# Two convolution blocks on one core: weight loads on another queue, an earlier comparison and table, one shared PSUM tile, and a half of the output summed by VectorE

## The chip, the cores and the metric

The kernel runs on 1 core of one Trainium2 chip. The core has TensorE (matmuls, results in PSUM), VectorE (DVE), ScalarE (ACT), GpSimd (POOL) and SyncE (SP), each with its own instruction stream that is executed in order, and 16 DMA engines that all of them share. The engines wait for each other by semaphores. The metric is the device time of one execution in microseconds. It is given as the median of 3 runs: 2735.2 us (2733.67 to 2737.22).

## The reference

The input `x` is 4 images of 256 channels of 48 x 48, float32. Two layers are added to it, each on a group-normalised copy (32 groups):

```python
x = x + _L0_conv_ref(_gn(x), ...)   # layer 0
x = x + _L1_conv_ref(_gn(x), ...)   # layer 1
```

Layer 0 is a 3x3 convolution with batch norm (given statistics) and ReLU, then 8-head attention over the 2304 pixels (32 channels a head, softmax over all pixels) and a projection:

```python
x = relu(bn(conv3x3(Vx, conv_w) + conv_b))
qkv = einsum('oc,bchw->bohw', qkv_w, x) + qkv_b
attn = softmax(einsum('bhdn,bhdm->bhnm', q, k) * scale)
out = einsum('oc,bchw->bohw', proj_w, einsum('bhem,bhnm->bhen', v, attn)) + proj_b
```

Layer 1 makes 45 guidance maps by a 3x3 convolution. In groups of nine, after a softmax, they weigh nine shifted copies of the input, at dilations 1, 6, 12, 24 and 36. The input and the five sums are mixed by a 1x1 convolution (256 x 1536), and the result `y` is normalised per channel with the mean and variance over all four images:

```python
for i, d in enumerate((1, 6, 12, 24, 36)):
    w = softmax(guidance[:, 9 * i:9 * (i + 1)], axis=1)
    outs.append(_dyn_branch(x, w, d))
y = conv1x1(concat(outs), W_scale)
return (y - mean) * rsqrt(var + EPS) * gamma + beta
```

So the output is x1 + (y * ysc + ysh), where x1 is the result of layer 0 and `ysc`, `ysh` are per channel and known only when `y` of all images is done.

## The kernel before, in words

A channel tile is `[128, 2, 2304]`: 128 partitions, two halves of 128 channels (`h` or `o`), all pixels of an image. Everything is float32. A pass over an image is cut into six chunks of 384 pixels.

**The first image.** Lines 557 to 560 issue four DMAs on SP's queue that load image 0 into `x_first`, 576 KB each. After some constants and memsets on POOL, line 2170 begins the first pass: seven DMAs on POOL's queue load the weights (`wc`, the convolution's, in two halves; then `wqkv`, `wp`, `vbc`, `wcat`, `wsc`), and twelve more on the same queue write zeros from `e1` to the margins of `w_d` in DRAM (line 2181). VectorE takes the statistics of the image as it lands (line 655), aggregates them (665), makes two sums on the first half of the weights (`weights.pair`, 786 and 787), and then finishes the group norm: `rstd_of` (97 to 99) adds EPS, ScalarE takes the root, VectorE the reciprocal. The image is normalised into `pads[0]`, the transform of the convolution (847 to 852) follows, and TensorE begins the convolution (962).

ScalarE needs a table for a function; another function can need another table. `table(func)` (line 610) runs the function on one column, so that the table is loaded there.

**The passes.** The loop at 2149 goes over b = 0..4. In pass b the layer 1 work of image b-1 (`dynamic_filters`) is interleaved with the convolution and the q, k, v of image b; then the attention of image b follows. In pass 4 no next image is left: `alone` is true, and the layer 1 work of image 3 is interleaved with `late()`, the 1x1 mixing of two chunks (4 and 3) of image 2 that were put off until then.

**The order within a pass is written by a planner**, at build time. Each piece of work is a generator in a list of streams: `loads`, `far`, `near` (the dilation of 1), `filters` (guidance maps and softmax), `mixes` (the 1x1 convolution), and `other`. A generator yields the time at which its next step is due. `drive` (1961) takes the first stream whose step is due by the planner's TensorE time; when none is due it takes a matmul from `other`. `clock(engine, ns, *after)` adds the cost of a step to an engine's planned time, and `slot(tag, bufs)` gives the planned time at which a buffer is free again. `moved` (1495) gives a copy to ScalarE or VectorE, whichever is free sooner by this plan. What the planner decides is fixed before the kernel runs; the engines then wait for each other by semaphores.

**Late chunks.** `late()` (1912) makes a PSUM tile `both` of two banks for each of the two chunks, in a pool with one buffer; each half gets 12 matmuls and is copied by ScalarE to `yl` (1934). The tile of the second chunk stands in the place of the first.

**The flag.** A bound on the attention scores is kept for each image and half; if one is over SAFE, a general version of the kernel runs afterwards. In pass 4 the stream `filters` calls `flag_of` (2077) before the third set of guidance maps: VectorE compares the bounds (`okay`), TensorE sums them into the PSUM tile `misc`, VectorE reduces them and writes `flag`. `misc` has one buffer, which the guidance maps and their transposes use too.

**The end.** `last_loads` (1944) is a stream that, once the last `near` work is issued, calls `table(AF.Sqrt)` and loads four chunks of `y` of image 2. After the last matmuls `finish` (2087) makes `ysc` and `ysh` (`batch_norm_of`, 161) and then the output, image by image: 0, 2, 3, 1. For images 0 and 1, `near_end` (2096) has ScalarE make y * ysc + ysh for the two parts of a half in place, and VectorE add it to x1; `y` lies by chunks of six rows apart (c, j), x1 by rows (j, c), so that each VectorE part reads from all chunks. For images 2 and 3, `far_end` (2116) has ScalarE shift x1, and VectorE add y * ysc in one scalar_tensor_tensor per chunk. SP issues the stores.

## Time and profile before

| What | Value |
|---|---|
| median of 3 runs (lowest, highest) | 2735.2 us (2733.67, 2737.22) |
| the profiled execution's own time | 2732.03 us |
| its span, first to last instruction | 2730.3 us |
| mean granted TensorE clock | 0.987 |
| first convolution matmul | 21.37 us |
| last matmul begins (four of L1897) | 2691.15 us |
| VectorE's last sum ends | 2722.15 us |

The profile is one execution of the program. The page gives the busy time of the engines and its share of the span; queries of the trace give the instructions in order of time (start, busy time, engine, line, operation, tiles and, in square brackets, the idle time of the engine before it and what ended it), and tables of who waited for whom (total time, how often, longest). A wait for several semaphores is put down to the one that came last. Matmuls are pipelined and their ends are modelled. PEld is TensorE's weight load; SPq is SyncE's queue.

### The profile page before, as it was taken

How to read it: one execution, taken by the hardware profiler on the slowest of the kernel's cores; microseconds unless marked ns; L12 is line 12 of the kernel's file. 1: busy time of each engine (PE TensorE's matmuls, PEld its weight loads, DVE VectorE, ACT ScalarE, POOL GpSimd, SP SyncE). 2: the span in 40 equal slices, each digit the busy share in tenths (PEclk: the TensorE clock that was granted, in tenths of full speed). 3: DMA queues.
4: the chain of work that ended last, by engine and by line, in shares of the span. 5: the costliest groups of instructions: out<-in, count | busy, mean ns of one | idle time of the engine just before them, and what ended most of it. 6: DMA issues, size and time to landing. Idle time of an engine off the chain costs nothing. (4 is left out here: it accounts for less than half of the span.)

```text
span 2730.3 us, 42450 instructions
## 1 busy us (share of the span) xinstructions
PE 2593.3 (95%) x16906; PEld 1091.3 (40%) x16906; DVE 2081.7 (76%) x2014; ACT 1806.0 (66%) x2273; POOL 810.3 (30%) x882
## 2 busy tenths in 40 slices
PE   6999999999999999999999999999989999999994
PEld 5632222555562222355554222245555222235452
DVE  7768888757739898857765988885875988885476
ACT  4479888634449888854446888884344988874344
POOL 5201100477520010068650001017764001000462
PEclk9999999999999999999999999999999999999997
DMA  4804445323252445433324344442325344432465
GB/s 171 225 13 105 108 98 108 90 61 107 63 104 59 99 93 110 99 80 86 90 57 84 86 105 100 102 99 74 94 69 136 99 93 96 103 82 75 114 192 182
DMA packets 137790, 273.67 MB, mean 100 GB/s; under 512 B 58104, under 2 KB 99744, under 8 KB 136688
## 3 DMA queue, kind: packets, MB, share of 16 engines
q0 software_dynamic: 25952, 135.74, 21.8%
q1 hardware_dynamic: 111632, 135.14, 18.6%
q8 instruction: 135, 2.21, 0.3%
q14 instruction: 71, 0.58, 0.1%
HBM read 112.12 MB, written 36.04 MB: 54 GB/s over the span
## 5 line engine op out<-in xcount | busy, mean ns | idle before, releaser
L1374 DVE TENSOR_TENSOR acc<-acc,p 128x2048 f32<-128x2048 f32 (+1 forms) x568 | 1052.1, 1852 | 119.8 <-ACT p L1334 70.0
L1334 ACT ACTIVATE p<-se 128x1536 f32<-128x1536 f32 x648 | 938.1, 1448 | 0.0
L1325 PE MATMUL so<-q,k 32*128 32x512 f32 (+1 forms) x1440 | 728.6, 593 | 18.8 <-ACT p L1333 16.3
L1325 PE MATMUL se<-q,k 32*128 32x512 f32 (+1 forms) x4320 | 737.3, 593 | 0.0
L1359 PE MATMUL num<-p,vT 128*32 128x512 f32 (+1 forms) x5760 | 711.3, 561 | 2.2 <-ACT ao L1384 2.2
L1333 ACT ACTIVATE p<-so 128x512 f32<-128x512 f32 x648 | 388.8, 600 | 193.8 <-PE se L1325 89.1
L1802 POOL TENSOR_TENSOR near<-near,prod 128x384 f32<-128x384 f32 x384 | 386.5, 1039 | 290.6 <-DVE prod L1796 281.7
L1325 PEld LDWEIGHTS so<-q,k 32*128 32x128 f32 x1440 | 216.7, 183 | 535.8 <-ACT p L1333 493.0
L1378 POOL DMA_DIRECT2D ring<-p x124 | 105.5, 851 | 775.2 <-ACT p L1334 486.3
L1359 PEld LDWEIGHTS num<-p,vT 128*32 128x32 f32 x5760 | 136.7, 108 | 480.0 <-issue 449.7
L1796 DVE TENSOR_TENSOR prod<-wb,pad 128x768 f32<-128x768 f32 x192 | 181.8, 954 | 92.3 <-ACT wb L1783 56.0
L1897 PE MATMUL py<-far,wsc 128*128 128x384 f32 x704 | 234.6, 487 | 0.0
L1783 ACT COPY wb<-ws 128x384 f32<-128x384 f32 x216 | 108.5, 506 | 183.1 <-DVE prod L1796 123.7
L1325 PEld LDWEIGHTS se<-q,k 32*128 32x128 f32 x4320 | 227.3, 183 | 4.9 <-ACT p L1334 3.9
L1376 POOL DMA_DIRECT2D ring<-p x32 | 17.9, 559 | 632.2 <-ACT p L1334 448.6
L1897 PEld LDWEIGHTS py<-far,wsc 128*128 128x128 f32 x704 | 132.0, 190 | 90.2 <-issue 2.5
L1498 ACT COPY far<-far 128x512 f32<-128x512 f32 x97 | 101.9, 1107 | 89.9 <-PE far L1730 86.6
L1530 PE MATMUL pg<-pad,wcat 128*45 128x384 f32 x864 | 146.5, 490 | 7.2 <-ACT lg L1588 7.0
L1249 PE MATMUL pq<-hid,wqkv 128*128 128x384 f32 x384 | 136.4, 510 | 15.0 <-ACT hid L1119 12.8
L1249 PEld LDWEIGHTS pq<-hid,wqkv 128*128 128x128 f32 x384 | 74.6, 198 | 70.7 <-ACT hid L1119 15.1
L1374 DVE TENSOR_TENSOR acc<-p,p 128x2048 f32<-128x2048 f32 x36 | 82.3, 2286 | 20.7 <-ACT p L1334 14.6
L1702 DVE COPY_PREDICATED amat<-along_y,bmat 128x768 f32<-128x768 uint32 x72 | 94.5, 1312 | 2.4
(311 smaller groups left out, 2686.7 us busy)
## 6 DMA issues: line engine op xcount, KB each, us to landing
ring<-p POOLq DMA_DIRECT2D x156, 768.0 KB, 5.7
ws<-w_d SPq DMA_DIRECT2D x216, 192.0 KB
ring<-u_d SPq DMA_DIRECT2D x36, 512.0 KB
pad<-in_x SPq DMA_DIRECT2D x14, 1152.0 KB
xst<-in_x POOLq DMA_DIRECT2D x36, 192.0 KB, 3.6
x_d<-pad SPq DMA_DIRECT2D x36, 192.0 KB
u_d<-pad SPq DMA_DIRECT2D x12, 512.0 KB
y_d<-y SPq DMA_DIRECT2D x13, 384.0 KB
```

What stands on the lines that cost most here:

```text
L1249: nc.tensor.matmul(pq[:, :CH], wqkv[:, i, s, g * P : (g + 1) * P], hid[:, i, cols], start=(i == 0), stop=(i == NH - 1),)
L1325: nc.tensor.matmul(dst[:, at : at + n], k_[r, g, m * P : (m + 1) * P], q[r, g, q0 : q0 + n], start=True, stop=True,)
L1333: nc.scalar.activation(p[:, 0, :], s1, AF.Exp, scale=QS)
L1334: nc.scalar.activation(p[:, 1:, :], s3, AF.Exp, scale=QS)
L1359: nc.tensor.matmul(st["num"][r, at : at + n], vT[:, m, g * P + j * D : g * P + (j + 1) * D], p[:, j, at : at + n], start=(m == 0 and not s ...
L1374: nc.vector.tensor_tensor(st["acc"][:, js], other[:, js], p[:, js], ALU.add)
L1378: nc.gpsimd.dma_start(out=extra, in_=p[:, 1:], accum_op=ALU.add)
L1530: nc.tensor.matmul(pg[64 * s : 64 * s + NG, :CH], wcat[:, ii, k, :], shifted(ii, cc, k // 3 - 1, k % 3 - 1), start=(i == 0 and k == 0), st ...
L1783: nc.scalar.copy(pw[:, :CH], fetched[c, k][0])
L1796: nc.vector.tensor_tensor(prod.rearrange("p h (r w) -> p h r w", w=WW), wb, src, ALU.mult)
L1802: nc.gpsimd.tensor_tensor(cat[:, h], cat[:, h], prod[:, h], ALU.add)
L1897: nc.tensor.matmul(py[c][:, o, :CH], wsc[:, n * NH + i, o * P : (o + 1) * P], rhs, start=(n == 0 and i == 0), stop=(n == order[-1] and i = ...
```

## The change

Five edits, in the order of the diff's places in the kernel's run:

1. A `table(AF.Sqrt)` is put at the start of ScalarE's work, and the seven weight loads go from POOL's queue to SP's, behind the four image loads. The twelve zero stores stay on POOL's queue.
2. The comparison of `flag_of` becomes a function of its own, `within`, called in the last image's pass after the attention's last projection; `flag_of` gets its result.
3. `late` makes one PSUM tile before its loop for both chunks, and the planner's line that waits for the slot goes.
4. The `table(AF.Sqrt)` of `last_loads` goes to the end of `filters`, with 1500 ns of ScalarE time in the plan.
5. In `near_end`, half 0 of image 0 is treated otherwise: VectorE makes x1 + y * ysc in eight scalar_tensor_tensor of 288 elements, ScalarE adds `ysh` in place after each two of them, and each quarter is stored.

```diff
         def table(func):
             t = small.tile([P, 1], F32, tag="table", name="table")
             nc.scalar.activation(t, one, func)
+
+        table(AF.Sqrt)
...
                     if alone and cs[0] == 2:
-                        flag_of(misc("pf")[:1, : B * NH])
+                        flag_of(misc("pf")[:1, : B * NH], okay)
                     yield from weights(cs)
+                if alone:
+                    table(AF.Sqrt)
+                    clock("ACT", 1500)
...
             def late():
 
+                both = ps_y.tile([P, 2, 512], F32, tag="y", name="pl")
                 for j, c in enumerate(LATE):
                     t = lates[j]
                     y = work1.tile([P, NH, CH], F32, tag="yl", name=f"yl_{c}", bufs=len(LATE))
                     y_2[c] = y
-                    both = ps_y.tile([P, 2, 512], F32, tag="y", name=f"pl_{c}")
-                    clock("PE", 0, slot("y", 1))
...
                     0.0 if NCK - 1 in near_done and (NCK - 2, "near") in mixed else NEVER
                 )
-                table(AF.Sqrt)
...
             table(AF.Sqrt)
+            if alone:
+                okay = within()
             for _ in norm.finish(misc):
...
-        def flag_of(pf):
+        def within():
             okay = small.tile([P, B * NH], F32, tag="okay", name="okay")
             nc.vector.tensor_scalar(
                 okay, bound.rearrange("p b g -> p (b g)"), SAFE, None, ALU.is_le
             )
+            return okay
+
+        def flag_of(pf, okay):
             nc.tensor.matmul(pf, one, okay, start=True, stop=True)
...
                 for o in range(NH):
+                    if (b, o) == (0, 0):
+                        y = ty[:, o].rearrange("p (c j w) -> p j c w", c=NCK, w=WW)
+                        n = N // SIDE
+                        for part in range(4):
+                            for j in (2 * part, 2 * part + 1):
+                                x1 = tx[:, o, j * n : (j + 1) * n].rearrange(
+                                    "p (c w) -> p c w", w=WW
+                                )
+                                nc.vector.scalar_tensor_tensor(
+                                    out=x1, in0=y[:, j], scalar=ysc[:, o : o + 1], in1=x1,
+                                    op0=ALU.mult, op1=ALU.add,
+                                )
+                            x1 = tx[:, o, 2 * part * n : 2 * (part + 1) * n]
+                            nc.scalar.activation(x1, x1, AF.Identity, bias=ysh[:, o : o + 1])
+                            nc.sync.dma_start(
+                                out=image(b, o)[:, 2 * part * n : 2 * (part + 1) * n], in_=x1
+                            )
+                        continue
                     half = N // 2
...
-                    parts = 4 if (b, o) in ((0, 0), (1, 1)) else 2
+                    parts = 4 if (b, o) == (1, 1) else 2
...
                         for h in range(NH):
-                            nc.gpsimd.dma_start(out=wc[:, h], in_=conv_w[:, h])
-                        nc.gpsimd.dma_start(out=wqkv, in_=qkv_w)
-                        nc.gpsimd.dma_start(out=wp, in_=proj_w)
-                        nc.gpsimd.dma_start(out=vbc, in_=v_b.rearrange("(h p) -> p h", p=P))
-                        nc.gpsimd.dma_start(out=wcat, in_=cat_w)
-                        nc.gpsimd.dma_start(out=wsc, in_=scale_w)
+                            nc.sync.dma_start(out=wc[:, h], in_=conv_w[:, h])
+                        nc.sync.dma_start(out=wqkv, in_=qkv_w)
+                        nc.sync.dma_start(out=wp, in_=proj_w)
+                        nc.sync.dma_start(out=vbc, in_=v_b.rearrange("(h p) -> p h", p=P))
+                        nc.sync.dma_start(out=wcat, in_=cat_w)
+                        nc.sync.dma_start(out=wsc, in_=scale_w)
```

## The prediction

> **What bounds the kernel now.** I read the page first, then the waits of TensorE and the timeline at the three places that the change touches: the first 25 us, the last image's pass (called the root here, 2480 to 2694 us) and the end. The page gives the bound.

> ```profile
> span 2730.3 us, 42450 instructions
> PE 2593.3 (95%) x16906; PEld 1091.3 (40%) x16906; DVE 2081.7 (76%) x2014; ACT 1806.0 (66%) x2273; POOL 810.3 (30%) x882
> ```

> TensorE is busy 95% of the span, 137 us idle. It first works at 21.4 us and last at 2692.7, so the head and tail are 21 + 38 = 59 us of that idle time. A microsecond counts only if it is taken from the head, from a wait of TensorE between, or from the tail. First the head, from the timeline:

> ```profile
> 11.28 1.48 DVE L655 BATCH_NORM_STATS2 stn<-x_first 128x6 f32<-128x384 f32 x3 [0.99 <-DMA x_first<-in_x]
> 12.60 0.52 POOL L2181 DMA_DIRECT2D w_d<-e  x1 [4.03 <-DMA wc<-in_conv_w]
> 13.07 0.90 DVE L786 TENSOR_TENSOR ring<-wc 128x768 f32<-128x768 f32 x1
> 14.52 1.28 ACT L98 ACT_TABLE_LOAD   x1
> 15.18 0.16 DVE L97 TENSOR_SCALAR gstd_n<-pv_n 128x2 f32<-128x2 f32 x1 [0.22 <-PE pv_n L680]
> 15.82 0.20 ACT L98 ACTIVATE gstd_n<-gstd_n 128x2 f32<-128x2 f32 x1
> 21.37 8.87 PE L962 MATMUL pc<-cv_q,ring 128*128 128x288 f32 x24 [6.23 <-DVE cv_q L851]
> ```

> The last quarter of the image lands at 11.28, the first half of the convolution weights just before 12.60. VectorE takes statistics, two sums on the weights (L786, L787), then the norm's root; from there it is hardly idle until TensorE starts. Next, TensorE's waits in the root:

> ```profile
> PE pf L2082 <- DVE okay L2079: 2.4, 1, 2.4
> PE pl L1924 <- ACT yl L1934: 2.2, 2, 1.6
> PE py L1897 <- ACT wqkv L1820: 1.2, 1, 1.2
> ```

> And the end, from the timeline:

> ```profile
> 2693.90 1.28 ACT L612 ACT_TABLE_LOAD   x1
> 2694.26 0.17 DVE L97 TENSOR_SCALAR ysc_f<-ymv 128x2 f32<-128x2 f32 x1
> 2695.30 0.19 ACT L98 ACTIVATE ysc_f<-ysc_f 128x2 f32<-128x2 f32 x1
> 2696.31 5.06 ACT L2102 ACTIVATE y<-y,ysh_f,ysc_f 128x1152 f32<-128x1152 f32 x4 [0.82 <-DVE ysh_f L173]
> 2698.93 5.30 DVE L2111 TENSOR_TENSOR x<-y,x 128x576 f32<-128x576 f32 x6 [2.46 <-ACT y L2102]
> 2716.84 5.31 DVE L2111 TENSOR_TENSOR pad<-y,pad 128x1152 f32<-128x1152 f32 x6
> 2718.23 6.78 SPq L2114 DMA_DIRECT2D out<-pad  x6
> ```

> From 2698.93 VectorE works without a gap to 2722.15. The stores follow it and fall a little behind: 590 KB take 1.44 us at 410 GB/s, and the windows show the DMA engines full from 2718 to 2726. So VectorE's start and its work set the end, the last stores add a fixed 8 us.

> **The change part by part.**

> *Weights behind the image, and the square-root table at the start.* Seven loads go from POOL's queue to SP's. SP has issued the four image loads by 2.78 and next waits for a store at 45.86, so nothing on SP is late. The DMA engines are full anyway (share 0.95 or more from 3 to 20 us, about 415 GB/s), and a load from SP alone already fills them (410 and 429 GB/s from 3 to 5 us). The image alone in front would land about 2 us sooner (1.3 MB of it is left at 5 us: 3 us at 415 GB/s, and 1.5 to land, so 9.5 against 11.28; the 1.5 is my estimate from image plus first weights, 3.55 MB, which the windows show moved by 11 us and the rows above landed by 12.6). But VectorE's next step, L786, needs weights, and image plus first weights are the same bytes. What is new is POOL: its twelve blank stores (L2181, 46.7 KB each) stood behind the weights, one issued at 7.99, the others from 12.60 to 26.7 each after a landing; now they follow the memsets at 4.1 us and run before the first weights have landed. Eleven more in front cost, by bytes, 11 x 46.7 KB / 415 = 1.24 us; by the window from 23.5 to 28.5 us, where five took 18% of 5 us, 11 x 0.18 = 2.0 us. The weights land at 13.8 to 14.55 instead of just before 12.60 (I take 12.55). L786 starts then, L97 follows 1.9 us later at 15.7 to 16.45 instead of 15.18. The table load between L97 and the root goes: the root starts 0.1 after L97's end (15.34 now) instead of at 15.82, which saves 0.38. Net +0.1 to +0.9; if the blanks don't push in (POOL's stores waiting their turn), L786 starts at 12.55 and the net is -1.1. I take +0.5, as the blanks' issue has nothing left to wait for. TensorE's first matmul moves with it, by VectorE's unbroken work.

> [...]

> *Flag compared first.* TensorE waits 2.39 us up to 2537.22 for `okay`, behind VectorE's queue, and 0.24 more for `count`. With `okay` made at about 2486 (0.2 us, in VectorE's idle time there) the flag's matmul still waits for its PSUM buffer, which ScalarE's copy L1588 leaves at 2536.29. `count` then follows the product that ends at 2536.95, and the next convolution starts near 2537.1 instead of 2537.66: -0.55. Bounds -0.6 and 0.

> *One PSUM tile for both put-off chunks.* TensorE's wait at 2518.20 (0.57) is between the chunks, the one of 1.64 at 2531.64 between two halves of one tile, and so is the one at 2691.15 (1.17, L1897 after L1820). So a matmul waits for the readers of the whole tile, also where the other half is read, and sharing the tile keeps the 0.57. What does change is the planner: the PE time loses a wait of 150 + 500 + 150 ns (0.8 us), so an order or two may differ. 0, with -0.6 and +0.6 as ends.

> *Root's table early.* It moves from 2693.90 to behind the copy L1588 that ends at 2586.20. At the end L98 starts 0.04 after L97, at 2694.47 instead of 2695.30: -0.83. In the middle 1.28 + 0.20 us go into ScalarE where it idles 1.20; its next copy moves from 2587.40 to about 2587.75. Queued behind are more copies out of PSUM, for which TensorE's `far` steps wait; but VectorE takes every other one. +0.2, between 0 and 1.5 (all of it). The planner is charged 1500 ns and will hand VectorE a copy more.

> [...]

> *First output half by VectorE.* The half (0,0) was 2 ScalarE passes (pitch 1.244) and 4 sums. Now 8 scalar_tensor_tensor of 288 elements start at once, at 2696.49, without the 2.46 us of idle. Their nearest row is L890 (128x288, 0.444 us); the L2128 rows start 0.087 sooner than their length, so a pitch of 0.36, and the last ends at 2696.49 + 7 x 0.36 + 0.44 = 2699.5. ScalarE shifts each quarter after its pair: 576 elements, 0.75 (between 0.68 from L847's 600 at 0.70 and L2120's 1152 at 1.24, and 0.82 from L2198). Here is the cost: ScalarE runs in order, and the passes for half (0,1) stand behind the four shifts. The last shift ends at 2699.55 + 0.75 = 2700.3, the two passes at 2700.25 + 1.24 + 1.33 = 2702.8. VectorE's sums for (0,1) start at 2702.87; they start at 2701.61 now. VectorE idles 3.3 us in the middle in place of 2.46 at the front, and all later work, gapless, moves by +1.3. Ends: +0.7 (pitch 0.30) and +2.6 (the 0.618 and pitch 0.53 of L2128). The stores wait for VectorE as before; the first one leaves earlier and ends early.

> **The sum.** +0.5 - 0.55 + 0 + 0.2 - 0.83 + 1.3 = +0.6 us. Against the profiled execution (2732.03, its span plus 1.7) that is 2732.6; this execution lies 3.2 under the median of the runs, so I forecast 2735.2 + 0.6 = 2735.8. The ends add to -2.4 and +4.8, rarely met together.

> **The rivals.**
> *The weights come in time* (blanks don't push in): the first part is -1.1, the sum -1.0, 2734.2. For it: they have small packets; against it: nothing holds POOL.
> *VectorE's half pays*: if (0,1) were ready when VectorE ends (0,0), its sums would start at 2699.9, 1.7 earlier than now, and the sum be -2.4, 2732.8. ScalarE's order is against it.
> *The planner's new order fits better*: TensorE idles 9 us in the root; it would need to win back six of them to count as faster, 2729.
> *Slower, by the planner's order*: its clock is 0.8 us early on TensorE and 1.5 late on ScalarE. In the put-off chunks TensorE already ran into late copies; one such wait is 1.2 to 2.4 us in the rows above. Three more, 1.8 each, are +5.4, so 2741.2; from three on it decides. Against it: after 2560 TensorE is full in nearly every window, with its inputs some 4 us ahead (`amat` done at 2665.5, used at 2669.3).

> **How the numbers follow.** Faster or slower means 0.2%, 5.5 us, about what a measurement of this kernel can tell. My sum: 0.60. Weights in time 0.14. VectorE's half pays 0.06. Better order 0.09. Slower order 0.11. The first three end within 0.2%: same 0.80, faster 0.09, slower 0.11. The range leaves out the two planner cases: 2731.0 is VectorE's half (2732.8) less the 2 us by which the runs scatter, 2740.0 the sum with all my upper ends (2735.2 + 4.8).

> **What would show it.** Right: L786 at 13.8 or later with a DMA wait before it, blanks all issued before 13 us, no table load at L98; the flag's matmul released by ScalarE, not `okay`; TensorE still waiting for L1934 between chunks; L98 right after L97; VectorE idle some 3 us for ScalarE before the sums of (0,1), and its end about 0.5 later, measured from the last matmul. Wrong: no such idle time, a first matmul before 21 us, or a root whose TensorE work from 2480 on is over 3 us longer or shorter.

## The result, and the profile after

| | median us (lowest, highest), runs | ratio to before, 95% interval |
|---|---|---|
| before, beside it | 2735.2 (2732.88, 2741.47), 11 | |
| changed | 2742.03 (2737.3, 2744.34), 11 | 1.0021 [1.0012, 1.0031] |
| changed, measured again (e5_after) | 2737.6 (2732.86, 2742.52), 12 | 1.0010 [0.9998, 1.0021] |

The forecast was 2735.8 us, no measurable difference. The first measurement lies above the range and just outside 0.2%, on the slow side; the second lies inside both. So two things need a cause: what the change costs, and why one kernel gives 1.0021 (5.7 us) and then 1.0010 (2.7).

The profiled execution of the changed kernel took 2742.76 us. Its page begins:

```profile
span 2740.9 us, 42455 instructions
PE 2597.5 (95%) x16906; PEld 1095.0 (40%) x16906; DVE 2085.1 (76%) x2018; ACT 1806.3 (66%) x2275; POOL 802.2 (29%) x875
```

The head, from the timeline (start, busy time, engine, line; in brackets the idle time before and what ended it):

```profile
4.04 4.12 POOL L2207 DMA_DIRECT2D w_d<-e  x8
9.52 1.47 DVE L657 BATCH_NORM_STATS2 stn<-x_first 128x6 f32<-128x384 f32 x3
12.61 0.96 DVE L788 TENSOR_TENSOR ring<-wc 128x768 f32<-128x768 f32 x1 [1.22 <-DMA wc<-in_conv_w]
14.47 0.15 DVE L97 TENSOR_SCALAR gstd_n<-pv_n 128x2 f32<-128x2 f32 x1
14.66 0.20 ACT L98 ACTIVATE gstd_n<-gstd_n 128x2 f32<-128x2 f32 x1 [1.93 <-DVE gstd_n L97]
20.27 8.08 PE L964 MATMUL pc<-cv_q,ring 128*128 128x288 f32 x24 [6.90 <-DVE cv_q L853]
30.60 4.62 PE L964 MATMUL pc<-cv_k,ring 128*128 128x288 f32 x11 [2.24 <-ACT m L908]
```

The image lands first now (statistics at 9.52 instead of 11.28), VectorE then waits 1.22 us for the weights, and the root follows L97 without a table load. TensorE begins 1.1 us sooner than in the profile of before. Its second group was released 1.1 us sooner as well (30.60 for 31.70), but it had idled 2.24 us, not 1.46.

TensorE's waits in the last image's pass (total, times, longest):

```profile
PE pl L1928 <- ACT yl L1938: 2.9, 2, 2.3
PE pf L2090 <- ACT lg L1590: 1.5, 1, 1.5
PE pg L1532 <- DVE count L2092: 0.5, 1, 0.5
```

The flag's matmul no longer waits for `okay` but for the copy that frees its PSUM tile. The wait in the put-off chunks has grown from 2.2 to 2.9. The end:

```profile
2703.92 0.17 DVE L97 TENSOR_SCALAR ysc_f<-ymv 128x2 f32<-128x2 f32 x1
2704.12 0.20 ACT L98 ACTIVATE ysc_f<-ysc_f 128x2 f32<-128x2 f32 x1 [0.56 <-DVE ysc_f L97]
2705.35 3.52 DVE L2115 SCALAR_TENSOR_TENSOR x<-y,ysc_f,x 128x288 f32<-128x288 f32 x8
2709.59 2.57 ACT L2128 ACTIVATE y<-y,ysh_f,ysc_f 128x1152 f32<-128x1152 f32 x2
2712.19 2.63 DVE L2137 TENSOR_TENSOR x<-y,x 128x1152 f32<-128x1152 f32 x2 [3.32 <-ACT y L2128]
2727.43 5.30 DVE L2137 TENSOR_TENSOR pad<-y,pad 128x1152 f32<-128x1152 f32 x6
```

The table is loaded by then, and VectorE's eight sums start at once; then it idles 3.32 us while ScalarE, in order, does four shifts before the passes of half (0,1). The last four matmuls start at 2700.82 and VectorE's last sum ends at 2732.73: 31.91 us, where it was 31.00. The tables below, like the expectations, use a longer measure: from the start of the very last matmul (2701.89) to the last record of VectorE's stream, its wait at the program's end (2740.86), which takes in the last stores. By it the tail is 38.97 us; it was 37.98.

The two profiled executions differ by 10.6 us, more than the medians. Taken apart by stages, 1.0 of that is the tail, 5.1 the granted clock (14 windows at half speed before the last matmul, 11 in before), and the rest comes in steps below 2 us in the attentions. Neither the clock nor these steps are in my sum.

### The profile page after: what moved, and what is told of

The parts are those of the page before. It is cut to its first block, busy times and chain, and to the rows that moved or that the text cites. A ratio compares the mean times of both kernels' runs of the same rounds, so it can differ in the third digit from the quotient of the medians.

```text
span 2740.9 us, 42455 instructions
## 1 busy us (share of the span) xinstructions
PE 2597.5 (95%) x16906; PEld 1095.0 (40%) x16906; DVE 2085.1 (76%) x2018; ACT 1806.3 (66%) x2275; POOL 802.2 (29%) x875
## 5 line engine op out<-in xcount | busy, mean ns | idle before, releaser
L1327 PE MATMUL so<-q,k 32*128 32x512 f32 (+1 forms) x1440 | 729.2, 594 | 20.8 <-ACT p L1335 18.4
```

The source lines that it names most:

```text
L1327: nc.tensor.matmul(dst[:, at : at + n], k_[r, g, m * P : (m + 1) * P], q[r, g, q0 : q0 + n], start=True, stop=True,)
```

## The experiments

Each was timed in five rounds; those told of together ran on one chip, beside the kernel before. Part n in the expectations is edit n. The theories: the change costs its tail (1 us) and the rest is chance; or the start, or the pass of the last image, costs more than I saw.

**e1 to e4: the kernel before again, and its parts alone.** Edits: none; edit 1; edit 5; edits 2 to 4.

> The kernel before, unchanged, timed against itself. All theories: a ratio of 1.000 within 0.1%. If the 5.7 us between before and after were scatter, this pair would also differ by 2 to 6 us and its trace would show another number of half-speed clock windows (11 in the profile of before, 14 in that of after). If the 5.7 us belong to the change, it stays within 2 us.

> Part 1 alone (weights on SP's queue, table at the start). Clock theory: the first matmul is 1.1 us earlier (20.27 instead of 21.37), the 24 matmuls end earlier still, TensorE then idles 2.2 us instead of 1.5 before the second group, and one 3.41 us window right after it runs at half speed; the head's net is +0.3 us by 35 us. If the lost 5 us come from here (the new phase of the work against the clock's windows), the whole is +3 to +5 us; if only the head counts, between -1.1 and +0.4. Rival, the root or the tail carries it: this kernel is within 1 us of before.

> Part 5 alone (VectorE's half of the output). Head and root are the instructions of before. Tail theory: the VectorE end moves by +0.9 + 0.8 = +1.7 us from the last matmul, as the table load still delays the start; whole +1.7 us. If the 5.7 us were all of the tail: +5. Clock theory: nothing upstream changes, so the half-speed windows number 11 give or take those of e1_same.

> Parts 2, 3 and 4 together (flag compared first, shared PSUM tile, root's table). Up to 2480 us the instructions are those of before. By my prediction's terms: -0.55 + 0.2 - 0.83 = -1.2 us. Rival, the planner's new order costs: the root's TensorE work from 2480 us to the last matmul is 2 us or more longer, whole +1 to +5 us. By the two traces so far the root gave +1.1 us from 2480 to the last matmul, so I would expect between -0.5 and +0.5 with the table's 0.83 gained at the end.

| | ratio, 95% interval | first matmul | last matmul to the program's end |
|---|---|---|---|
| e1_same | 0.9999 [0.9986, 1.0012] | 21.86 | 37.98 |
| e2_start | 1.0004 [0.9992, 1.0017] | 20.46 | 38.04 |
| e3_tail | 0.9994 [0.9982, 1.0007] | 20.47 | 39.80 |
| e4_root | 0.9998 [0.9984, 1.0012] | 20.27 | 37.14 |

No part shows by itself in the times: single executions of the kernel before run from 2727.5 to 2746.0 us here, a standard deviation of 4.5. The traces are sharper. The tail is the same to 0.1 us wherever its code is the same: VectorE's half costs 1.82, the early table gives 0.84. To VectorE's last sum the differences are the same. And the first matmul starts anywhere from 20.27 to 21.86 with the *old* start, so the 1.1 us that I read as the gain of edit 1 was chance. With five traces of each start the new one is 0.3 us sooner, give or take 0.35 (standard errors here and below).

**The clock's windows.** In all traces TensorE's granted clock is either 1.000 or 0.500, in windows of 3413.3 ns on a fixed grid, and the grid's place differs per execution (0.44, 1.12, 2.03, 2.37, 2.41, 3.14 us in the first six). In the ten traces without fillers 7814 such windows can be judged. In 77 TensorE was busy below 42%, and the next window was at half speed after every one. Of the 631 between 42% and 89% it happened after 48, and above that never. The 42% is read off these windows: the least busy one without a slow follower had 42.5%. So 2 us of idle time within one window are enough (58% of 3413.3 ns is 1.98 us). The kernel has eight places behind the head where TensorE idles 1.99 to 6.11 us in every trace. Seven are the same in all ten; the eighth is the flag's wait (2.39), or with edits 2 and 3 the one of the put-off chunks (2.27 to 2.29). How the grid falls on them is chance.

**e5 to e8: the changed kernel again, without edit 1, without edit 5, and with another order on ScalarE.** The last one's edit, in the first output image:

```diff
                     if (b, o) == (0, 0):
+                        scaled(ty, 1)      # the two ScalarE passes of half (0,1)
...
-                            nc.scalar.activation(x1, x1, AF.Identity, bias=ysh[:, o : o + 1])
...
+                        shifted(2)         # two of the four shifts; two more in far_end of image 2
```

> The changed kernel again, beside the kernel before on one chip. The single parts gave 1.0004 (start), 0.9994 (tail), 0.9998 (root), each within 0.13%, which add to nothing, where the whole had given 1.0021. Theory 1, the whole costs little: in the traces only the tail differs each time by the same amount (38.97 us from the last matmul to VectorE's end, 37.98 in both traces of before); the rest was the luck of the clock's windows. Then +1 to +3 us, 1.0004 to 1.0011. Theory 2, the parts together do more than alone: again 1.0015 to 1.003.

> The changed kernel with part 1 undone. Theory 1: within 1 us of the changed kernel; tail again 39.0 us, first matmul anywhere between 20.3 and 21.9 us, as in the four traces with the old start. Theory 2 with the start at fault: 3 us or more faster than the changed kernel.

> The changed kernel with part 5 undone. From the last matmul to VectorE's end 37.1 us (as in the run of parts 2 to 4), 1.8 less than the changed kernel; whole -1.8 us against the changed kernel by theory 1. If the tail were the fault of more, -4 us.

> The changed kernel, with ScalarE's order in the first output image changed: the two passes of half (0,1) go ahead of the four shifts of half (0,0), and the last two shifts behind the first two passes of image 2. If VectorE's idle 3.32 us comes from ScalarE's order, as I forecast, it goes to below 0.5, some 1.2 us come back before the sums of image 2, and VectorE ends about 2.1 us sooner from the last matmul: 36.9 instead of 39.0 us. If the stores or VectorE's own work set the end, 38 us or more, or the span moves by less than half of that.

| | ratio, 95% interval | last matmul to the program's end |
|---|---|---|
| e5_after | 1.0010 [0.9998, 1.0021] | 38.96 |
| e6_no_start | 1.0001 [0.9990, 1.0011] | 38.91 |
| e7_no_tail | 1.0003 [0.9990, 1.0015] | 37.21 |
| e8_order | 1.0000 [0.9986, 1.0014] | 36.12 |

In e8 the idle time of 3.32 us before the sums of half (0,1) is gone, as the timeline shows:

```profile
2696.82 2.58 ACT L2110 ACTIVATE y<-y,ysh_f,ysc_f 128x1152 f32<-128x1152 f32 x2 [0.82 <-DVE ysh_f L173]
2697.02 3.52 DVE L2132 SCALAR_TENSOR_TENSOR x<-y,ysc_f,x 128x288 f32<-128x288 f32 x8
2700.46 2.62 DVE L2148 TENSOR_TENSOR x<-y,x 128x1152 f32<-128x1152 f32 x2
2706.68 1.68 DVE L2166 SCALAR_TENSOR_TENSOR x<-yp,ysc_f,x 128x384 f32<-128x384 f32 x3 [0.36 <-ACT x L2157]
```

The tail is 2.84 us shorter than in the changed kernel, where I expected 2.1. So ScalarE's order was what edit 5 cost.

The second measurement of the changed kernel is 3.9 us below the first (means 2737.66 and 2741.53). Its mean granted clock is 0.9862, that of the first 0.9849; 0.0013 of 2740 is 3.6 us. The first eleven executions had met more slow windows.

**e9 to e12: the idle places filled.** Fillers of 256 columns go into six of the eight places, into a PSUM tile that real matmuls overwrite next; what is computed does not change:

```diff
                     relus(max(clock.t["ACT"], clock.t["PE"]))
+                    if t == 0 and n == 0 and b < B:
+                        busy(m, 8)
...
+                        if fill:
+                            coming_pq = psum_tile(f"pq_{b}_{c}_{g}_1")
...
+                            if fill and i:
+                                busy(coming_pq, 18 if b == B - 1 else 8)
```

> The kernel before, with filler matmuls (8 of 256 columns, 0.24 us each, into a PSUM tile that the next real matmuls overwrite) in six of the eight places where TensorE idled over 1.9 us in every trace: before the first transformed matmul of images 1 to 3 (2.3 us idle) and before the second matmul of their first q (2.95, 2.95 and 6.1 us; 18 fillers in the last). Clock theory: a window of the 3.413 us grid in which TensorE idles some 2 us makes the next window half speed, and where the grid falls decides; so the windows at half speed go from 10 to 17 before the last matmul to about 3 to 6, 8 to 13 us of granted clock come back, and the times scatter less (4 us before). Rival, the clock windows only show idle time that is lost anyway: same time within 2 us.

> The same fillers, and part 1 (start). The runs so far put part 1 at about +2.2 us (2740.3 against 2737.9, and 2737.7 against 2735.6 with and without it), which no place of the traces shows. If it is a real cost, this is 2 us slower than the fillers alone; if it was the luck of the windows, within 1 us of them or 0.4 us faster (the first matmul).

> The changed kernel with the same fillers. If the change costs its tail alone, +1 us against the fillers alone (0.5 with a sooner first matmul, 1.5 with a wait more in the root); if the 3.9 us that the two measurements of the changed kernel gave on average are real, +3 to +5 us.

> The changed kernel without part 1, with ScalarE's order as in the run of that order, and the fillers. The order gave 36.12 us from the last matmul to VectorE's end instead of 37.98: 1.9 us faster than the fillers alone, and 8 to 14 us faster than the kernel before, if the clock theory holds; 1 to 2 us faster than before, if not.

| | ratio, 95% interval | mean us | mean clock |
|---|---|---|---|
| before, beside them | | 2737.3 | 0.9862 |
| e9_busy | 0.9967 [0.9954, 0.9979] | 2728.3 | 0.9906 |
| e10_busy_start | 0.9974 [0.9960, 0.9989] | 2729.8 | 0.9908 |
| e11_busy_after | 0.9972 [0.9960, 0.9984] | 2730.1 | 0.9907 |
| e12_best | 0.9955 [0.9937, 0.9973] | 2724.5 | 0.9913 |

Work that does nothing makes the kernel 9 us faster. Two stretches of the kernel before, by windows (length; busy time of PE, PEld, VectorE, ScalarE and POOL; granted clock, DMA share, GB/s):

```profile
730.00:750.00 20.00, 17.05 (x58) 9.29 (x57) 11.37 (x13) 7.90 (x13) 9.07 (x10) 0.83 0.19 41
2018.00:2034.00 16.00, 9.10 (x21) 5.03 (x20) 9.46 (x9) 5.67 (x10) 10.96 (x9) 0.68 0.08 15
```

and the like in e9:

```profile
730.00:750.00 20.00, 20.00 (x82) 12.65 (x81) 13.18 (x17) 9.50 (x16) 11.01 (x12) 1.00 0.25 55
2010.00:2030.00 20.00, 18.32 (x86) 13.98 (x86) 14.34 (x18) 9.33 (x18) 13.15 (x11) 1.00 0.09 22
```

The clock stays at 1.00 there. Of the clock the runs gained 0.0044, 12 us of TensorE's time, and 9 reached the end. The times of e9 and e11 also scatter less: their standard deviations are 1.8 and 2.3 us, that of the kernel before beside them is 4.3. The fillers also move TensorE's instruction stream, which can matter by itself (e18 below); but ScalarE's waits over 0.6 us for the attention's DMAs sum to 19.4 us in e9 and to 18.2 to 20.8 in the five traces with the old start and no fillers, so the gain does not come from there. On this ground the changed kernel is 1.8 us slower (e11 against e9, bootstrap 0.3 to 3.5). The tail explains 1.0. Edit 1 alone gives +1.5, from -1.2 to 4.4 (e10 scatters by 4.8), which decides nothing. e12 is 3.8 us faster than e9, twice what the order's 1.9 foretold; it also has edits 2 to 4.

**e13 to e16: which half of edit 1.** Three pairs with and without edit 1 had differed by 2.4, 2.1 and 1.5 us. On e12, the quietest kernel, its halves make a square:

> The kernel with fillers, the new ScalarE order and the old start, as the base of a square of four on one chip: 2724.5 us again (its runs scattered by 1.3 us, a third of the others), within 1 us.

> The base, with the seven weight loads on SP's queue alone. If part 1 costs some 2 us and the queue is why: +2 us against the base, and +2 between both and the table alone. If part 1 costs nothing: within 1 us, the first matmul between 20.2 and 21.0 us.

> The base, with the square-root table loaded at the start alone. The load of 1.28 us between L97 and L98 goes: the root starts 0.1 us after L97 instead of 0.64. -0.5 us against the base, if nothing gives it back; 0 if the second group's wait at 28 us takes it; +2 if the table is what costs in part 1.

> The base with all of part 1. If the +2 us of the three earlier pairs is real: 2726.5 us and the sum of the two halves. If it was the clock's windows: within 1 us of the base.

| | old start's table | table at the start |
|---|---|---|
| loads on POOL's queue | e13: 0.9953 [0.9940, 0.9967], 2724.1 us | e15: 0.9941 [0.9928, 0.9955], 2721.3 us |
| loads on SP's queue | e14: 0.9964 [0.9950, 0.9977], 2726.8 us | e16: 0.9966 [0.9953, 0.9978], 2727.4 us |

From the four means the queue costs 4.4 us (bootstrap 3.1 to 5.8) and the table gives 1.1 (-0.3 to 2.4). The two do not simply add: the queue costs 2.7 without the early table and 6.1 with it, and the table gives 2.8 with the old queue and nothing clear with the new (+0.6, from -1.3 to 2.3). But SP has issued the loads by 7.8 us. Aligning TensorE's instructions over the four filled traces of each queue, the last scores of the attentions (2474 us) come 4.1 us later, give or take 1.5. The first matmul is 0.3 of that; a good part lies in a few places of the attentions, each the same in all traces of one queue. At 508 us the new queue gains 1.05 us by a wait that only the old one has, at 878 it loses 1.06, between 1680 and 1720 2.8. There, in e14 (timeline):

```profile
1702.31 0.60 ACT L1344 ACTIVATE p<-so 128x512 f32<-128x512 f32 x1 [2.59 <-DMA ring<-p]
1702.95 0.84 PE L1336 MATMUL so<-q,k 32*128 32x512 f32 x1 [2.13 <-ACT p L1344]
```

and, by windows, just after it:

```profile
1703.40:1706.80 3.40, 3.40 (x20) 0.52 (x16) 2.42 (x2) 2.78 (x3) 0.20 (x1) 0.50 0.87 173
```

The same step in the timeline of e15:

```profile
1700.07 0.60 ACT L1346 ACTIVATE p<-so 128x512 f32<-128x512 f32 x1 [0.64 <-DVE acc L1387]
1700.72 0.69 PE L1338 MATMUL so<-q,k 32*128 32x512 f32 x1 [0.18 <-ACT p L1346]
```

In the attention POOL issues DMAs that add three quarters of `p` to `ring`, and ScalarE can't write that buffer of `p` again before they land. In e14 one landed late, ScalarE waited 2.59 us, TensorE 2.13, and the next window ran at half speed (0.50). POOL's issue of that DMA, and of the one at 501 us, in e14 (timeline):

```profile
501.40 0.87 POOL L1389 DMA_DIRECT2D ring<-p  x1 [8.14 <-ACT p L1345]
1694.65 0.87 POOL L1389 DMA_DIRECT2D ring<-p  x1 [6.19 <-ACT p L1344]
```

and in e15:

```profile
501.48 0.87 POOL L1391 DMA_DIRECT2D ring<-p  x1 [9.22 <-ACT p L1346]
1693.54 0.85 POOL L1391 DMA_DIRECT2D ring<-p  x1 [5.38 <-ACT p L1347]
```

In e15 the DMA before had landed and ScalarE's part was written by 1693.23, and POOL began the issue 0.31 us later. In e14 both were there by 1693.51, and it began 1.14 us later. Such late issues stand at fixed places, and the queue alone decides where. POOL usually begins an issue 0.49 us after its wait for the DMA before ends, or 0.28 us after ScalarE's write, whichever is later. In all eleven traces with the old queue the first of these is 1.85, 1.23 and 1.23 us near 1044, 1652 and 2456 us, and the second 1.35 near 502 us. In all nine with the new queue the first is 0.79, 1.53 and 1.23 near 224, 875 and 1695 us, and the second 1.66 near 1117 us. So the waits at 508 and 878 us are POOL's late issues. The loads were 768 of the 25952 packets of POOL's queue, and three of the four late issues come near the same counts with both, behind 8816, 12560 and 17312 packets with the old queue and 8768, 12944 and 17264 with the new. What in POOL's issue takes the time is not shown.

Between 1680 and 1720 something is added. The DMA queues while that accumulation was under way (packets, MB, share), and its time from issue to landing, in e14:

```profile
q0 software_dynamic: 144, 0.79, 53.1%
q8 instruction: 1, 0.02, 0.8%
ring<-p POOLq DMA_DIRECT2D x1, 768.0 KB, 7.5
```

and in e15:

```profile
q0 software_dynamic: 144, 0.79, 61.8%
q8 instruction: 1, 0.02, 0.9%
ring<-p POOLq DMA_DIRECT2D x1, 768.0 KB, 6.4
```

A packet of instructions, 16 KB in one piece, shares the 16 DMA engines (the 0.8% and 0.9% above). In all four filled traces with the old queue it starts 5.93 or 5.94 us after the issue and the accumulation takes 6.42 or 6.43; in all four with the new one it starts 4.99 to 5.46 after the late issue, and the accumulation takes 7.33 to 7.55. There are 135 such packets in the kernel before, one at every 128 of TensorE's 16906 matmuls or so, so this is TensorE's stream (with the 16906 weight loads counted, 250 instructions a packet). Of the ten traces without fillers, all 147 accumulations over 6.4 us had such a packet under way; in the profile of before, none without an instruction packet or other traffic took over 5.78.

The records of TensorE's sequencer hold 231 entries in the kernel before and 234 in every kernel with the loads on SP's queue (230 and 233 with the fillers): three semaphore instructions more, near TensorE's 502nd, 3480th and 3580th matmul. When I ran e17 and e18 I held that these move the packets. At 1700 us the traces say otherwise: the packet starts at TensorE's matmul 10670 to 10674 in all eight, and what came later was POOL's issue.

That does not close the account of the queue. Summed over the eight places of late issues, the new queue is 2.1 us slower in the filled traces, give or take 0.6, and 1.6 faster, give or take 0.5, in the ten without fillers, where the issue at 1695 us meets no packet. So in the filled kernel about half of the 4.1 us is found there, and the cost of about 2 us without fillers has no place in these traces.

**e17 and e18: the stream moved, no queue touched.** These test whether the place of TensorE's stream matters at all. On e15, two or sixteen matmuls of two columns more, in TensorE's idle time at 14 us:

```diff
+                        if (b, at, g, o) == (0, 0, 0, 0):
+                            for _ in range(16):
+                                nc.tensor.matmul(
+                                    pc[:, :2], ident, ident[:, :2], start=True, stop=True
+                                )
```

> The run of the table alone (2721.3 us, queue as in the kernel before) with two matmuls of two columns more in TensorE's stream, in its idle time at 14 us, so that nothing waits for them. Theory: the queue edit costs because it adds three semaphore instructions to TensorE's stream, so that the stream's fetches (one packet of 16 KB for every 128 matmuls) fall beside other accumulations of the attention, and an accumulation beside such a packet takes 6.4 to 7.6 us instead of 5.7 and holds ScalarE. Four instructions more should do the like: the wait of 1.05 us at 507 us that all eight traces with the old queue have should go or move, waits should come up elsewhere (878, 1699 us), and the time change by 1 to 4 us. Rival, the queue itself costs (who issues the loads): same waits, same time within 1 us.

> The same with sixteen matmuls (32 instructions, an eighth of a 16 KB packet). Fetch theory: the fetches fall 16 matmuls sooner, half a step of the attention, so most of the waits listed for the old queue (507, 1076, 1658, 2462 us) change places; the time moves by up to 4 us in either direction. Rival, the queue itself: same waits, same time within 1 us.

e17: 0.9959 [0.9944, 0.9975]; e18: 0.9977 [0.9965, 0.9989]; e15, their base, 0.9941 [0.9928, 0.9955]. In e18 the accumulations over 6.4 us are 15 as in e15, and not one of them is the same; all have a packet beside them, and ScalarE's waits over 0.6 us for them grow from 17.3 to 23.0 us in sum. Thirty-two instructions in an idle stretch cost about 0.36%, 10 us by the ratios to the kernel before (e15 ran on another chip). The wait at 508 us stayed (1.5), and POOL's late issues stand where they stand in e15, so there I was wrong: that wait does not hang on TensorE's stream. e17 says less: waits mostly where e15 has them, 508 included, against my expectation, and an interval that overlaps e15's. So the place of the stream matters; but a moved stream is not what the queue's waits at 508, 878 and 1700 us come from.

The fastest is e15: fillers, the new order on ScalarE, edits 2 to 5, the table at the start and the loads on POOL's queue. It is 16 us (0.59%) faster than the kernel before, and faster than the changed kernel.

## Why the prediction was wrong

*Weights behind the image* (+0.5, blanks in front of the weights). Wrong in the mechanism. Eight blanks were issued by 8.2 us, as I said, but L788 started at 12.61 (12.57 to 13.39 in the five traces without fillers), not 13.8. The rival "the weights come in time" was right here; but its gain of 1.1 was not there either, for L786 starts at 11.98 to 13.56 with the old queue. I took one execution's 13.07 for a constant. My 415 GB/s "from 3 to 20 us" also holds to 14 us only; from there the windows show 334 and 380.

*The step that failed* is the sentence "nothing on SP is late", with which I closed the account of the queue. I looked at the queue that the loads go to, and at POOL only up to 26.7 us; what the move does to POOL's later issues I put at nothing without a reason. POOL issues three quarters of `p` 156 times after that, and the move shifts which of them it begins late, by up to 1.4 us each. The queue costs 4.4 us on the filled kernel, and edit 1 about 2 in three other pairs; no term or rival of mine has it. About half of it is found at these places in the filled kernel; where the 2 us of the kernel without fillers arise stays open. My nearest rival, slower by the planner's order, named another place (the last image's pass), which the traces with and without edits 2 to 4 show unchanged (218.3 and 218.7 us from the last scores to the last matmul with the half-speed time taken off, give or take 0.5).

*Table at the start* (-0.38): -1.1 (-2.4 to 0.3) in the square, but +0.6 (-1.3 to 2.3) beside the new queue, which is the case I forecast. The runs don't decide it; the table load is gone from L98, as I said.

*Flag* (-0.55): the waits went from 2.39 + 0.24 to 1.52 + 0.53, -0.58. Right, by the step named: released by the copy, not by `okay`.

*One PSUM tile* (0, ends ±0.6): the 0.57 between the chunks stayed, as argued. The planner's new order made the wait within the second one 2.29 instead of 1.64: +0.65, at my upper end.

*Root's table* (-0.83 at the end): 37.98 became 37.14, -0.84. Nothing is seen of the +0.2 in the middle.

*VectorE's half* (+1.3): +1.82, or 1.75 beside the early table. The mechanism is as predicted, and e8 shows it. The term was mis-sized by the pitch of the eight sums: 0.44 us (3.52 for eight), not 0.36; 7 x 0.08 = 0.56.

With the measured sizes the five edits' own places sum to -0.3 - 0.58 + 0.65 - 0.84 + 1.82 = +0.75, where I had +0.6. That this is near is luck: the first term is 0.8 lower than mine, and the two others that I missed are 0.65 and 0.5 higher. Added to that come the 2 us or so of edit 1 and the luck of the windows. There the range failed too: it has 2 us for scatter below and none above, while single executions vary with a standard deviation of 4.1 (81 runs, correlation -0.75 with the granted clock), and the two measurements of the changed kernel lie 3.9 apart. The first one met more slow windows and left the range; the second, with 2.7 us, lies in it.

## What to carry to other kernels

When a DMA moves to another queue, follow the queue that it leaves to the end of the kernel, not only the one that it joins: here POOL's late issues moved to other places, the same in every execution. A wait that returns at the same place in all traces of a kernel is not chance. In a loop that leans on large DMAs, look also for instruction packets beside them. Look for places where TensorE idles 2 us or more outright and fill them with matmuls that nobody reads; it was worth 9 us here, more than all five edits together. Before a trace is compared with another, compare two traces of the same kernel: the head's "gain" of 1.1 us was smaller than the 1.6 by which the old start varies.
